# Ten of 64 context projections of a cross-attention moved into an expert layer's scatter and gather, and kept in HBM

## The chip, the cores and the metric

The kernel runs on one core of a Trainium2 chip, in one launch. The metric is the device time of the core in microseconds. The engines are TensorE (PE, with its weight loads listed as PEld), VectorE (DVE), ScalarE (ACT), GpSimd (POOL) and SyncE (SP), which only issues DMAs here.

## The reference

Two transformer layers run on 8 sequences of 100 tokens with 512 features (800 tokens), with a context of 8 x 722 rows. Everything is float32.

```
x = x + xattn0(layernorm(x), ctx)      # 16 heads of 32; causal: only the first 100 context rows count
x = x + experts0(layernorm(x))         # 8 experts of 2048, the best 2 per token, GELU
x = x + xattn1(layernorm(x), ctx)      # 16 heads of 64, below
x = x + experts1(layernorm(x))         # 8 experts of 1024, the best 2 per token, SiLU gate

xattn1:  q = xn @ Wq;  k, v = xn @ Wkv
         mem = ctx @ Wm                # 512 -> 1024; serves as keys and as values
         attn = softmax(q . [k, mem] / 8);  out = (attn . [v, mem]) @ Wo + bo
```

The part that matters is `mem = ctx @ Wm`. It depends on the context and on a weight alone, not on anything that earlier stages compute.

## The kernel before, in words

The kernel is written with a tile framework that places the semaphores and orders the instructions of each engine; the order in which they run is not always that of the source. Tiles come from pools. Tiles of one tag share `bufs` places, and a new tile waits until the old one in its place has been read for the last time. Memory of a closed pool is given to the next pool in the same way.

The stages run one after the other:

1. First attention (L407 to L513). `cT` (the context), `kT` and `v` are its large tiles in the pool `ap`. The last part of the stage (L535 to L550) is the output projection, the layer norm and the router's logits for each of seven tiles of tokens.
2. Routing (L552 to L573). `places` ranks the tokens of each expert. `owners` reads the order of the experts into SP's registers, since the weights' addresses depend on it. `weights.load` then fetches the first two weight tiles, and `send` scatters the rows to HBM with 14 indirect DMAs on POOL.
3. First expert layer (L576 to L623). `work_off` goes through eight jobs, one per expert. `arrive` loads the rows (`xg`) and turns them, `hidden` and `product` are the two matmul stages, and `send_back` (the function `returned`) stores the answers. `weights.get` keeps loads seven tiles ahead on SP. Behind the jobs stands `rest` (L378), a branch that every engine passes and that is taken only when an expert overflows. Then 28 indirect gathers (`fetch`, L317) add the answers to `x` (L621).
4. Second attention (L626 to L778). After a layer norm (L634 to L638) come the queries `qT` (L645), and then 64 units, 8 batches times 8 blocks `ic` of two heads each. Batch 0 and batch 4 begin with the keys `kT` for four batches, and each batch with its `v` (L750) and with the load of its context `cb` (L739).
5. Second expert layer (L781 to L869), built as the first.

In a unit of the second attention, `keys` (L649) projects 128 columns of `mem` for all 722 context rows: 2 halves of 4 accumulating matmuls (L655), each evicted by ScalarE (L661). The result `mT` has features on partitions. `values` (L664) turns it with six PE transposes (L671) and three VectorE copies into `mv`, with rows on partitions. `weighed` (L679) makes scores (L689), the maximum (L693) and the exponentials (L695). `turned` transposes the probabilities (L710 to L716) and `attended` multiplies them with `mv` (L725 to L734). The loop is staggered by one unit:

```
mT = keys(cb, ic)
if before is not None:
    turn = turned(*before[4])
mv = values(mT)
here = b, ic, v, mv, weighed(b, ic, kT, mT)
if before is not None:
    attended(*before[:4], *turn)
```

Of the kernel before, what the change touches and what calls it, by code (L numbers as in the profile page):

```python
# [8 lines left out]
F32 = mybir.dt.float32  # L9
# [4 lines left out]
P = 128  # L14
D = 512
DC = D // P
B, T, S = 8, 100, 722
NT = B * T
HALF = NT // 2
NTILE = -(-NT // P)  # L20
# [4 lines left out]
IC = INNER // P  # L25
# [3 lines left out]
NKH = NK // 2  # L29
EPS = 1e-5  # L30


# [30 lines left out]
def two_layers(ctx: ExitStack, tc: tile.TileContext, a: dict, out: bass.AP):  # L63
# [151 lines left out]
    sent = dram.tile([ROWS, D], F32, name="sent")  # L215
    answers = dram.tile([ROWS, D], F32, name="answers")

    def places(at1, at2, pool, psum, tag, name):
# [145 lines left out]

    def work_off(jobs, arrive, hidden, product, send_back, first=None):


        (x, raw), done = arrive(*jobs[0][:3]), None
        if first is not None:
            weights.load(first + 8, raw)  # L370
        for k, (e, r0, n, w1, w2) in enumerate(jobs):
            h = hidden(e, n, x, w1, lambda: done and send_back(*done))
            if k + 1 < len(jobs):
                x, _ = arrive(*jobs[k + 1][:3])
            done = e, r0, n, product(e, n, h, w2)
        send_back(*done)
# [16 lines left out]
    def columns_part(dst, xT, w, h, c, psum, evict):  # L393
# [8 lines left out]
        evict(dst[:, c, cols], ps[:, :HALF])  # L402


    f0 = ctx.enter_context(ExitStack())
    fp = f0.enter_context(tc.tile_pool(name="f0", bufs=1))
    with tc.tile_pool(name="a0", bufs=1) as ap, tc.tile_pool(name="a0w", bufs=3) as aw, tc.tile_pool(  # L407
        name="a0s", bufs=1, space=bass.MemoryType.PSUM
    ) as ps_s, tc.tile_pool(name="a0p", bufs=2, space=bass.MemoryType.PSUM) as ps:
        w_q = weights.get(0, 0)  # L410
        cT = ap.tile([P, DC, B, T], F32, name="cT")
        for dc, queue in enumerate((nc.gpsimd, nc.gpsimd, nc.sync, nc.sync)):
# [7 lines left out]
        make_causal_mask(nc, mask, -1e30)  # L420
        nil = ap.tile([P, 1024], F32, name="nil")
        nc.gpsimd.memset(nil, 0.0)
# [15 lines left out]
        qT = ap.tile([P, DC, NT], F32, name="qT0")  # L438
        kT = ap.tile([P, DC, NT], F32, name="kT0")
        v = ap.tile([T, B, D], F32, name="v0")  # L440

# [84 lines left out]
        nc.vector.tensor_tensor(wg0, wg0, gamma0.unsqueeze(2).to_broadcast([P, DC, NE]), ALU.mult)  # L526
        xl = fp.tile([P, NTILE, D], F32, name="xl0")
        xT = ap.tile([P, DC, NT], F32, tag="xT", name="xTf0")
# [31 lines left out]
        weights.load(W_L0F + 2)  # L560
        send(xl, where, "f0")
        b1s = by_order(hot, b1.rearrange("p e f -> p f e"), F0 // P, fp, "b1")
        b2s = by_order(hot, b2T, DC, fp, "b2")
# [12 lines left out]
    with f0, tc.tile_pool(name="f0w", bufs=2) as fw, tc.tile_pool(  # L576
        name="f0p", bufs=2, space=bass.MemoryType.PSUM
    ) as ps:
        NF = F0 // P

        def hidden0(e, n, xg, w1, between):
            h = fw.tile([P, NF, CAP], F32, tag="h", name="h0")
            for g in range(NF // 4):
# [13 lines left out]

        def work0(jobs, first=None):
            work_off(
                jobs, lambda e, r0, n: arrived(e, r0, n, fw, ps, gamma0, beta0), hidden0,  # L600
                lambda e, n, h, w2: products(n, h, [w2(g) for g in range(NF // 4)], NF, fw, ps, b2s[:, e, :]),
                lambda e, r0, n, yT: returned(e, r0, n, yT, fw, ps), first,
            )
# [6 lines left out]
            for e in range(NE)  # L610
        ], W_L0F)
        rest(
            more, work0, lambda piece, e, g: piece(of(0, "W1", e, g)), lambda piece, e, g: piece(of(0, "W2", e, g)), 4
        )

        for i in range(NTILE):
            w = rows[i]
# [8 lines left out]
    with tc.tile_pool(name="a1", bufs=1) as ap, ExitStack() as later, tc.tile_pool(  # L626
# [21 lines left out]

        def keys(cb, ic):  # L649

            mT = aw.tile([P, S], F32, tag="mT", name="mT")
            for h in range(2):
                pm = ps.tile([P, 512], F32, tag="tp", name="ps_m")
                for dc in range(DC):
                    nc.tensor.matmul(  # L655
                        pm[:, : S // 2],
                        w_m[ic // 4][:, dc, (ic % 4) * P : (ic % 4 + 1) * P],
                        cb[:, dc, h * (S // 2) : (h + 1) * (S // 2)],
                        start=dc == 0, stop=dc == DC - 1,
                    )  # L660
                nc.scalar.copy(mT[:, h * (S // 2) : (h + 1) * (S // 2)], pm[:, : S // 2])  # L661
            return mT

        def values(mT):  # L664

            mv = aw.tile([P, NSC, P], F32, tag="mv", name="mv1")
            for c0, c1 in ((0, 4), (4, NSC)):
                pt = ps.tile([P, 4, P], F32, tag="tp", name="ps_mv")
                for c in range(c0, c1):
                    w = min(P, S - c * P)  # L670
                    nc.tensor.transpose(pt[:w, c - c0, :], mT[:, c * P : c * P + w], ident)  # L671
                if c1 < NSC:
                    nc.vector.tensor_copy(mv[:, c0:c1, :], pt)
                else:
                    nc.vector.tensor_copy(mv[:, c0 : c1 - 1, :], pt[:, : c1 - 1 - c0, :])
                    nc.vector.tensor_copy(mv[:SLAST, c1 - 1, :], pt[:SLAST, c1 - 1 - c0, :])
            return mv
# [79 lines left out]
        for n in range(B * IC):  # L757
            b, ic = divmod(n, IC)
            if ic == 0:
                cb, kT, v = batch(b, kT)  # L760
            mT = keys(cb, ic)
            if before is not None:
                turn = turned(*before[4])
            mv = values(mT)
            here = b, ic, v, mv, weighed(b, ic, kT, mT)
# [174 lines left out]
```

## Time and profile before

| what | value |
|---|---|
| median of three runs | 1920.64 us (1918.02 to 1923.47) |
| the profiled execution | 1925.57 us, its span 1923.5 us |
| instructions | 26011 |
| mean granted TensorE clock | 0.944 of full |
| PE busy | 1731.2 us (90% of the span) |
| VectorE, ScalarE, POOL busy | 583.6, 459.8, 153.8 us |
| DMA | 203.19 MB, mean 106 GB/s |

The page of a profile gives busy time per engine, then the span in 40 slices of some 48 us with the busy share of each engine in tenths, the granted TensorE clock, and the DMA share. Groups of instructions are named by line, engine and operation, with the tiles that they write and read. A view of windows gives the busy time of each engine in chosen stretches. A timeline lists instructions in order of time; in brackets stands the idle time before one and what ended it. The stages lie about here: first attention to 210 us, routing and scatter to 247, expert jobs to 635, gather and layer norm to 682, second attention to about 1510, second expert layer to the end.

### The profile page before, as it was taken

How to read it: one execution, taken by the hardware profiler on the slowest of the kernel's cores; microseconds unless marked ns; L12 is line 12 of the kernel's file. 1: busy time of each engine (PE TensorE's matmuls, PEld its weight loads, DVE VectorE, ACT ScalarE, POOL GpSimd, SP SyncE). 2: the span in 40 equal slices, each digit the busy share in tenths (PEclk: the TensorE clock that was granted, in tenths of full speed). 3: DMA queues.
4: the chain of work that ended last, by engine and by line, in shares of the span. 5: the costliest groups of instructions: out<-in, count | busy, mean ns of one | idle time of the engine just before them, and what ended most of it. 6: DMA issues, size and time to landing. Idle time of an engine off the chain costs nothing. (4 is left out here: it accounts for less than half of the span.)

```text
span 1923.5 us, 26011 instructions
## 1 busy us (share of the span) xinstructions
PE 1731.2 (90%) x10442; PEld 1312.4 (68%) x10442; DVE 583.6 (30%) x1409; ACT 459.8 (24%) x1359; POOL 153.8 (8%) x262
## 2 busy tenths in 40 slices
PE   4999389999999289999999999999999939999990
PEld 2455179999999255666666656666666428999990
DVE  2465410011110411444444424444434221111115
ACT  2364111111111022333333323333333010010110
POOL 2000210000000310000000000000000040000003
PEclk9997689999999689999999999999999959999995
DMA  9800274545554520000000000000000046455623
GB/s 334 334 2 1 106 265 167 188 177 193 210 200 190 170 84 22 1 32 1 32 6 27 32 1 1 32 7 26 1 1 1 11 166 249 166 189 200 209 80 111
DMA packets 44202, 203.19 MB, mean 106 GB/s; under 512 B 8490, under 2 KB 8618, under 8 KB 27938
## 3 DMA queue, kind: packets, MB, share of 16 engines
q1 hardware_dynamic: 27904, 158.54, 22.5%
q0 software_dynamic: 8992, 27.93, 4.2%
q10 hardware_dynamic: 7170, 14.91, 2.3%
q8 instruction: 86, 1.41, 0.3%
q14 instruction: 50, 0.41, 0.1%
HBM read 162.21 MB, written 39.13 MB: 105 GB/s over the span
## 5 line engine op out<-in xcount | busy, mean ns | idle before, releaser
L655 PE MATMUL ps_m<-cb,w 128*128 128x361 f32 x1024 | 327.0, 471 | 0.0
L341 PE MATMUL ps_y<-h,w 128*128 128x256 f32 (+7 forms) x1536 | 280.5, 344 | 0.0
L341 PEld LDWEIGHTS ps_y<-h,w 128*128 128x128 f32 x1536 | 268.6, 190 | 7.9
L655 PEld LDWEIGHTS ps_m<-cb,w 128*128 128x128 f32 x1024 | 188.9, 189 | 114.1 <-issue 4.6
L589 PE MATMUL ps_h<-xgT,w 128*128 128x256 f32 (+7 forms) x1024 | 188.8, 345 | 0.0
L589 PEld LDWEIGHTS ps_h<-xgT,w 128*128 128x128 f32 x1024 | 180.2, 191 | 5.7 <-ACT h L593 0.2
L695 ACT ACTIVATE pr<-ps_sc,m 100x822 f32<-100x822 f32 x128 | 120.0, 943 | 194.8 <-DVE m L693 194.8
L711 DVE COPY prT<-ps_ptA 128x500 f32<-128x500 f32 x128 | 82.0, 679 | 232.2 <-PE ps_ptA L710 232.1
L693 DVE TENSOR_REDUCE m<-ps_sc 100x1 f32<-100x822 f32 x128 | 123.8, 1009 | 45.8 <-PE ps_sc L689 45.8
L593 ACT ACTIVATE h<-ps_h,s_b 128x256 f32<-128x256 f32 (+7 forms) x128 | 56.1, 439 | 303.6 <-PE ps_h L589 303.6
L661 ACT COPY mT<-ps_m 128x361 f32<-128x361 f32 x128 | 59.2, 462 | 246.4 <-PE ps_m L655 246.4
L398 PE MATMUL ps_col<-xT,w 128*128 128x400 f32 x320 | 116.0, 521 | 0.0
L819 PE MATMUL ps_g<-xgT,w 128*128 128x256 f32 (+7 forms) x512 | 104.3, 347 | 0.0
L819 PE MATMUL ps_u<-xgT,w 128*128 128x256 f32 (+7 forms) x512 | 102.8, 344 | 0.0
L398 PEld LDWEIGHTS ps_col<-xT,w 128*128 128x128 f32 x320 | 62.3, 198 | 46.5 <-issue 5.1
L819 PEld LDWEIGHTS ps_g<-xgT,w 128*128 128x128 f32 x512 | 91.3, 192 | 3.0
L819 PEld LDWEIGHTS ps_u<-xgT,w 128*128 128x128 f32 x512 | 90.7, 190 | 2.7
L689 PE MATMUL ps_sc<-mT,qT 64*100 64x311 f32 (+1 forms) x512 | 89.2, 466 | 0.0
L719 POOL COPY wide<-sums 100x128 f32<-100x128 f32 x64 | 19.0, 296 | 779.9 <-DVE sums L700 779.9
L731 PE MATMUL ps_av<-prT,mv 128*64 128x100 f32 (+1 forms) x1536 | 80.6, 253 | 0.0
L825 DVE TENSOR_TENSOR h<-ps_u,sg 128x256 f32<-128x256 f32 (+7 forms) x64 | 24.3, 380 | 183.8 <-PE ps_u L819 183.8
L824 ACT ACTIVATE sg<-ps_g 128x256 f32<-128x256 f32 (+7 forms) x64 | 22.3, 349 | 238.8 <-PE ps_g L819 238.8
(219 smaller groups left out, 1853.1 us busy)
## 6 DMA issues: line engine op xcount, KB each, us to landing
w<-in_W SPq DMA_DIRECT2D x64, 1024.0 KB, 6.6
w<-in_w_gate SPq DMA_DIRECT2D x16, 1024.0 KB, 4.8
w<-in_w_up SPq DMA_DIRECT2D x16, 1024.0 KB, 7.3
w<-in_w_down SPq DMA_DIRECT2D x16, 1024.0 KB, 6.7
sent<-nil SPq DMA_DIRECT2D x25, 512.0 KB, 10.1
cb<-in_ctxT ACTq DMA_DIRECT2D x8, 1444.0 KB, 6.2
answers<-nil SPq DMA_DIRECT2D x19, 512.0 KB, 9.9
xg<-sent POOLq DMA_DIRECT2D x18, 256.0 KB, 4.8
```

The costliest lines, as they stand in the source:

```text
L341: nc.tensor.matmul(py[:, k, :n], ws[f // 4][:, f % 4, dc * P : (dc + 1) * P], h[:, f, :n], start=f == 0, stop=f == nf - 1,)
L398: nc.tensor.matmul(ps[:, :HALF], w[c // 4][:, dc, (c % 4) * P : (c % 4 + 1) * P], xT[:, dc, cols], start=dc == 0, stop=dc == DC - 1,)
L589: nc.tensor.matmul(ph[:, :n], w[:, dc, j * P : (j + 1) * P], xg[:, dc, :n], start=dc == 0, stop=dc == DC - 1,)
L593: nc.scalar.activation(h[:, f, :n], ph[:, :n], AF.Gelu, bias=b1s[:, e, f : f + 1])
L655: nc.tensor.matmul(pm[:, : S // 2], w_m[ic // 4][:, dc, (ic % 4) * P : (ic % 4 + 1) * P], cb[:, dc, h * (S // 2) : (h + 1) * (S // 2)], st ...
L661: nc.scalar.copy(mT[:, h * (S // 2) : (h + 1) * (S // 2)], pm[:, : S // 2])
L689: nc.tensor.matmul(sc[:, bank, c0:c1], qT[r, ic, q0 : q0 + T], keys_, start=True, stop=True)
L693: nc.vector.tensor_reduce(m, sc[:, :, :NKH], AX.XY, ALU.max, negate=True)
L695: nc.scalar.activation(pr.rearrange("p (a n) -> p a n", a=2), sc[:, :, :NKH], AF.Exp, bias=m, accum_out=sums[:, j : j + 1],)
L711: nc.vector.tensor_copy(prT[:, : NSC - 1, :], pt)
L731: nc.tensor.matmul(po[r, 0, :], vj, prT[j][:w, c, :], start=c == 0, stop=c == NSC)
L819: nc.tensor.matmul(p_[:, :n], w_[:, dc, j * P : (j + 1) * P], xg[:, dc, :n], start=dc == 0, stop=dc == DC - 1,)
```

## The change

For batches 0 and 1, the blocks `ic` = 0, 1, 3, 5 and 7 are done early, ten units in all. Their `mT` and `mv` go to two tensors in HBM, `kept_keys` and `kept_values`, by ScalarE's DMA queue. In the second attention these units load both back on SP in place of projecting and turning; `mv` needs two loads, since the last of its six row blocks has 82 rows.

Batch 0's five projections stand in the source after `send`. Their weights and context are loaded on SP into the places of `cT`, `kT` and `v`. Batch 1's five stand after `rest`, ahead of the gathers. Their weights and context are loaded by POOL from inside job 4 of the expert layer, behind one-element copies that wait for a row tile. For the memory, the expert layer's `h` has one buffer in place of two. In the second attention, where a kept unit is followed by one that is not kept, half of the next unit's projection is placed in the kept unit.

```diff
+EARLY = ((0, 1, 3, 5, 7), (0, 1, 3, 5, 7))
+KEPT = {(b, ic): (b * len(EARLY[0]) + k) for b in range(len(EARLY)) for k, ic in enumerate(EARLY[b])}
...
+    def moved(dma, mv, kept, store):
+        for part in ((slice(0, P), slice(0, NSC - 1)), (slice(0, SLAST), slice(NSC - 1, NSC))):
+            here, there = mv[part[0], part[1], :], kept[part[0], part[1], :]
+            dma(out=there if store else here, in_=here if store else there)
+
+    def project_early(b, cb, w_m, tiles, psum, tags):
+        for ic in EARLY[b]:
+            mT, mv = tiles()
+            context_columns(mT, ic, cb, w_m, psum, tags[0])
+            nc.scalar.dma_start(out=kept_keys[KEPT[b, ic]], in_=mT)
+            context_rows(mv, mT, psum, tags[1], nc.scalar.copy)
+            moved(nc.scalar.dma_start, mv, kept_values[KEPT[b, ic]], True)
...
         owners(0, experts)
         weights.load(W_L0F + 2)
         send(xl, where, "f0")
+        w_m = []
+        for g, tag in enumerate(("cT", "kT")):
+            w_m.append(ap.tile([P, 4, 512], F32, tag=tag, name=f"wm0{g}"))
+            nc.sync.dma_start(out=w_m[g], in_=a["Wm"][g])
+        cb = ap.tile([P, DC, S], F32, tag="v", name="cb0")
+        nc.sync.dma_start(out=cb, in_=a["ctxT"][:, 0, :].rearrange("(c p) s -> p c s", p=P))
+        project_early(
+            0, cb, w_m, lambda: (
+                ap.tile([P, S], F32, tag="nil", name="mT0", bufs=2), aw.tile([P, NSC, P], F32, tag="xn", name="mv0")
+            ), ps, ("tp", "av"),
+        )
...
+        def fetch_context(behind):
+
+            for t, src in (
+                (w_m[0], a["Wm"][0]), (w_m[1], a["Wm"][1]),
+                (cb, a["ctxT"][:, 1, :].rearrange("(c p) s -> p c s", p=P)),
+            ):
+                nc.gpsimd.tensor_copy(t[:1, 0, :1], behind[:1, 0, :1])
+                nc.gpsimd.dma_start(out=t, in_=src)
...
-            h = fw.tile([P, NF, CAP], F32, tag="h", name="h0")
+            h = fw.tile([P, NF, CAP], F32, tag="h", name="h0", bufs=1)
...
+        project_early(
+            1, cb, w_m, lambda: (
+                fw.tile([P, S], F32, tag="xgT", name="mT1"), fw.tile([P, NSC, P], F32, tag="xg", name="mv1")
+            ), ps, ("m", "tp"),
+        )
         for i in range(NTILE):
             w = rows[i]
...
+            if (b, ic) in KEPT:
+                nc.sync.dma_start(out=mT, in_=kept_keys[KEPT[b, ic]])
+            else:
+                context_columns(mT, ic, cb, w_m, ps, "tp", (0, 1) if first and whole else (0,) if first else (1,))
             return mT
...
+            if (b, ic) in KEPT:
+                moved(nc.sync.dma_start, mv, kept_values[KEPT[b, ic]], False)
+            else:
+                context_rows(mv, mT, ps, "tp", nc.vector.tensor_copy)
             return mv
...
-            mT = keys(cb, ic)
+            mT = keys(b, ic, cb)
+            if (b, ic) in KEPT and ic + 1 < IC and (b, ic + 1) not in KEPT:
+                keys(b, ic + 1, cb, whole=False)
             if before is not None:
                 turn = turned(*before[4])
-            mv = values(mT)
+            mv = values(b, ic, mT)
```

`context_columns` and `context_rows` are the former bodies of `keys` and `values`, with the halves and the engine of the copies as arguments.

## The prediction

> **What bounds the kernel now.** I read the page first, for which engine is busy in which slice, then windows cut at the stage borders, then TensorE's timeline inside one unit of the second attention.
>
> ```profile
> PE 1731.2 (90%) x10442; PEld 1312.4 (68%) x10442; DVE 583.6 (30%) x1409; ACT 459.8 (24%) x1359; POOL 153.8 (8%) x262
> PE   4999389999999289999999999999999939999990
> PEclk9997689999999689999999999999999959999995
> ```
>
> PE is busy 90% of the span, and full in every slice but a few. Its holes are the strips where tokens are routed, scattered or gathered; the clock row dips in the same places. The change moves PE work out of a full stretch into two of the holes, so the windows (columns: window, length, then busy us of PE, PEld, DVE, ACT, POOL, clock, DMA share, GB/s) have to show how much hole there is:
>
> ```profile
> 175.00:208.00 33.00, 29.82 (x126) 16.94 (x124) 15.13 (x56) 11.07 (x24) 0.00 (x0) 1.00 0.00 0
> 208.00:217.00 9.00, 1.94 (x17) 1.72 (x17) 5.72 (x38) 2.53 (x5) 0.00 (x0) 0.55 0.00 0
> 217.00:225.00 8.00, 0.57 (x3) 0.38 (x2) 7.17 (x26) 0.00 (x0) 0.53 (x1) 0.50 0.00 0
> 225.00:244.00 19.00, 0.00 (x0) 0.00 (x0) 0.00 (x0) 0.00 (x0) 13.02 (x14) 0.50 0.77 284
> 640.00:669.00 29.00, 0.49 (x3) 0.52 (x4) 15.51 (x32) 0.98 (x4) 15.18 (x14) 0.50 0.56 168
> 750.00:1500.00 750.00, 749.19 (x5157) 488.93 (x5156) 311.43 (x602) 249.19 (x716) 18.96 (x64) 1.00 0.04 13
> ```
>
> From 750 to 1500, the second attention, PE is idle for 0.8 us in 750 and the clock is 1.00: a matmul taken out there comes off the time. In the routing and scatter strip (208 to 244) and the gather strip (640 to 669) PE stands still at clock 0.50. The DMA engines are empty until 225, then 77% busy.
>
> TensorE inside the second attention (start, busy, engine, line, tile):
>
> ```profile
> 998.31 0.87 PE L671 MATMUL ps_mv<-ident,mT 128*128 128x128 f32 x6
> 999.12 0.42 PE L689 MATMUL ps_sc<-kT,qT 64*100 64x100 f32 x4
> ...
> 1000.68 0.31 PE L725 MATMUL ps_av<-ident,wide 100*128 100x100 f32 x1
> ...
> 1002.28 5.12 PE L655 MATMUL ps_m<-cb,w 128*128 128x361 f32 x16
> 1007.24 0.59 PE L710 MATMUL ps_ptA<-ident,pr 100*128 100x100 f32 x5
> ...
> 1011.30 0.30 PE L725 MATMUL ps_av<-ident,wide 100*128 100x100 f32 x1
> ```
>
> A unit takes 1011.30 - 1000.68 = 10.62 us. The projection (L655) holds PE from 1002.28 to 1007.24, 4.96 us by start to start; its turning (L671) from 998.31 to 999.12, 0.81 us. Together 5.77 us.
>
> **Part 1, what is removed.** Ten units lose both: 10 x 5.77 = 57.7 us. The work also covered a wait. The scores of a unit end as 1000.68 begins, and its softmax rows come from these two:
>
> ```profile
> 1001.89 0.95 ACT L695 ACTIVATE pr<-ps_sc,m 100x822 f32<-100x822 f32 x1 [3.03 <-DVE m L693]
> 1002.83 0.94 ACT L695 ACTIVATE pr<-ps_sc,m 100x822 f32<-100x822 f32 x1
> ```
>
> They are there at 1002.84 and 1003.77. PE has `attended` of the unit before (1000.68 to 1002.28), then the projection, then `turned`, which needs them. Without a projection PE would wait to 1002.84, turn the first (0.6), and wait 0.3 again: 0.9 us. At ic = 1, 3 and 5 the change puts half of the next projection (2.5 us) there, and at ic = 0 the batch's values (L750, 6.9 us from 748.69 to 755.55) stand there; only ic = 7 is bare: 2 x 0.9 = 1.8 us. Net **-55.9 us**. VectorE loses three copies in each of these units and ScalarE two, but both have slack (311 and 249 busy us of 750), so I cost that at nothing.
>
> **Part 2, the loads back.** Each of the ten units puts three loads on SP, 370, 328 and 42 KB, 30 in all. SP does nothing between the second `Wo` load (issued at about 727.7) and the end of this stage. The first is needed when scores start, about 755. Later ones may start when the tile two units back is freed and are needed about 14 us on (a step of some 8 us and most of one of 7). Nearest rows: a 1024 KB weight lands in 6.6 us, a 1444 KB `cb` in 6.2. A load that waits on SP holds up only later loads of this kind. Taken: 0. Bounds: no gain is possible; the cover ends at a landing of 14 us, and each us beyond costs up to 10.
>
> **Part 3, five projections in the scatter strip.** PE needs 5 x 5.77 = 28.9 us at full clock. What decides is when they may start. `wm` and `cb` lie in the places of `cT`, `kT` and `v`, free after the last `attended0` (about 170); DMA is idle there, so 3.5 MB land by about 177. But in the code their SP loads stand after `owners` and two weights, which issue at 225.43. Does the order on an engine follow the code? No:
>
> ```profile
> 163.18 0.41 PE L480 MATMUL ps_pt<-ident,pr 100*100 100x100 f32 x1
> 163.38 1.96 PE L541 MATMUL ps_o<-w,qT 128*128 128x512 f32 x2
> 165.13 0.37 PE L480 MATMUL ps_pt<-ident,pr 100*100 100x100 f32 x1
> ```
>
> Output projections (L541) run between transposes of attention units that the code puts before them, and the `cb` load of L739 is issued at 689.78 among the evictions of L647. Instructions are ordered by when their inputs are ready, so I take the loads and matmuls to move ahead. Then the cover is PE's idle time from 177 to the first `xg` transposes at 247.43: about 3 + 7.1 + 7.4 + 22.4 = 40 us, against 28.9 us. Slots of 0.3 us may push routing matmuls back: +1 (0 to 5). The stores, 5 x 0.74 MB on ScalarE's queue, fall partly into 225 to 244: some 2.2 MB at the 378 GB/s this trace reaches are 5.9 us, where 23% of 19 = 4.4 us are free: +1. ScalarE has 5 x (2 x 0.46 + 1.1) us of copies and 15 issues of some 0.4, all below PE's 28.9. Taken: **+2 us**; bounds -3 (experts starting on a warm clock) and +8.
>
> **Part 4, fetching for batch 1.** Three copies and three DMA issues on POOL inside the expert layer. POOL idles 15 to 30 us between its issues there, and one copy with one issue is about 1 us. Behind them on POOL stand the `answers` stores and `xg` loads, issued 17 to 30 us apart. The 3.5 MB run beside weights at some 190 GB/s; with 150 left they need 24 us, and weights are loaded seven ahead. `h` with one buffer: PE has finished `product` before the next `hidden` writes it. Taken: 0; bounds 0 and +3.
>
> **Part 5, five projections in the gather strip.** The last matmul before the strip ends at 634.84, the next is at 668.51. PE passes a branch first. ScalarE's row shows what a branch costs and what a cold clock costs:
>
> ```profile
> 614.54 0.41 ACT L593 ACTIVATE h<-ps_h,s_b 128x176 f32<-128x176 f32 x1 [0.78 <-PE ps_h L589]
> 620.37 1.28 ACT L133 ACT_TABLE_LOAD   x1 [5.42 <-ACTq L381]
> ...
> 687.09 0.50 ACT L647 ACTIVATE qT<-ps_col 128x400 f32<-128x400 f32 x1 [4.28 <-PE ps_col L398]
> 689.78 0.50 ACT L647 ACTIVATE qT<-ps_col 128x400 f32<-128x400 f32 x1 [2.18 <-PE ps_col L398]
> ```
>
> 5.42 us at the branch puts PE's start at 640.3. By then the clock is at 0.5: the first `qT` group took 681.5 to 687.0, 5.4 us, the next 2.69, so a cold start costs 2.7 us. The Trainium skill (TensorE: Matmul & The Clock Gate, Part 1: The HAM clock gate) speaks against work put into such a strip: after an idle window of about 3.4 us PE runs at half rate, and needs about 3.4 us of sustained work to recover, a loss of 1.7 us. I take the row, 2.7, as it is this place; with the rule the total would be 1.0 less. Were the clock never to recover, each group would cost 57.7 us. End on PE: 640.3 + 28.9 + 2.7 = 671.9.
>
> ScalarE's copies wait on PE there, and behind them stand the square roots of the next layer norm (first at 653.03), for which VectorE waits; they cost nothing as long as the strip ends on PE anyway. Then the next stage must get its memory: `xn` at 667.87 and the `bo` load at 667.96 both came just after the last reader of the old buffers (667.73). Now the last store must land too: copies and issue, 1.5 us, then the landing. By the skill (DMA: Bandwidth & Descriptors, Anatomy of one DMA) about 2.0 us plus bytes over 436 GB/s, 2.9 us for 370 KB, an estimate; the trace's nearest row, `answers<-y` into HBM, 256 KB, has 6.6, on a busier queue. They give 676.3 and 680.0, that is +8.6 or +12.3 against 667.73, or only +3.4 if the memory does not overlap. Taken: **+8 us**, near the rule, because DMA is emptier at the end of the strip; the row would make the total 4 more. Bounds -3 (`qT` on a warm clock) and +14.
>
> **Sum.** -55.9 + 2 + 8 = -45.9. The profiled execution took 1925.57 us (span 1923.5, 2.1 around it): 1879.7. The median of the runs is 1920.64, 4.9 lower: **1875**.
>
> **The rivals.** (a) Half saved: kept units wait on softmax or loads, some 2 us each, 20 in all: 1895. For it: VectorE and ScalarE need 3.1 us between scores and probabilities. Against it: 4 us of cover in eight of ten units. (b) In series: the loads keep their place behind `owners`. Weights 2.1, scatters 3.3 and context 3.5 MB at some 365 GB/s from 225.4 end at about 250; 28.9 + 2.7 + 3 us on PE and to store put the first `xg` transposes at 284.6, 37 us late in place of 2: 1910. For it: the code's order. Against it: the rows above. (c) Slower: as (b), and the clock stays at 0.50 as in those windows, since PE waits on copies between matmuls. Then 57.7 us from 250 and 3 to store end at 311, 64 late: 1937. It decides once the first experts start more than 48 us late, after 295. Against it: the clock was back at 1.00 by 256 when L589 began. (d) Nothing changes: if gaps gave back all 56 us by chance, about 1921.
>
> **How the numbers follow.** Main case 0.66 (own range 1860 to 1888), (a) 0.13, (b) 0.10, (c) and mishaps of its size 0.08, (d) 0.03. The range 1859 to 1908 takes in the low bounds, (a) and half of (b); outside stay (c), (d), half of (b) and a little below. About 0.3% (6 us) is what a measurement can tell from no change. Faster is main, (a) and (b), 0.89; same 0.03; slower 0.08.
>
> **What would show it.** Right: projection matmuls starting near 177 to 210 and ended before 245; first `xg` transposes by 252; clock 1.00 from 210 to 238; ten units of about 5 us (or pairs of half) less; the first `qT` matmul at about 690. Wrong: `wm` and `cb` loads after 225; PE waiting on DMA `mT` or `mv` in the kept units; transposes of `xn` after 690; probabilities as releaser of `turned` in more than the two bare units.

## The result, and the profile after

The changed kernel takes 1889.26 us (median of four runs, 1887.25 to 1891.05), the kernel before 1921.31 us in the same comparison. The ratio is 0.9834, with a 95% interval from 0.9817 to 0.9852: 32 us are gone. The forecast was 1875 us, in a range from 1859 to 1908. Its direction and range held; the gain is 14 us smaller than its point.

First the page of the changed kernel, the same three rows as were shown of before.

```profile
PE 1738.8 (92%) x10442; PEld 1315.2 (70%) x10442; DVE 572.9 (30%) x1379; ACT 468.5 (25%) x1389; POOL 154.6 (8%) x268
PE   4999969999999979999999999999999939999990
PEclk9997889999999979999999999999999959999995
```

PE's instruction count is unchanged, 10442: nothing was saved, work was moved. The two dips are the holes. In the fifth and sixth slice, the scatter strip, the PE row has 9 and 6, where it had 3 and 8; in the 14th and 15th, the gather strip, it has 9 and 7, where it had 2 and 8. The windows at the same borders as before (window, length, then busy us of PE, PEld, DVE, ACT, POOL, clock, DMA share, GB/s), with two added behind the borders, since both strips end later now:

```profile
208.00:217.00 9.00, 9.00 (x24) 4.97 (x24) 4.71 (x32) 2.26 (x5) 0.00 (x0) 0.51 0.00 0
217.00:225.00 8.00, 8.00 (x35) 5.23 (x34) 3.57 (x16) 2.40 (x6) 0.00 (x0) 1.00 0.21 81
225.00:244.00 19.00, 16.51 (x68) 10.36 (x66) 3.63 (x11) 6.42 (x18) 11.79 (x12) 1.00 0.86 319
244.00:256.00 12.00, 0.58 (x3) 0.61 (x4) 0.00 (x0) 1.28 (x1) 4.71 (x12) 0.50 0.71 254
640.00:669.00 29.00, 22.25 (x81) 14.35 (x80) 7.88 (x15) 6.07 (x15) 11.32 (x12) 0.88 0.78 264
669.00:686.00 17.00, 11.60 (x48) 7.26 (x46) 8.87 (x19) 4.78 (x14) 3.99 (x4) 0.95 0.61 218
```

PE fills the holes. Three things are new beside that. From 208 to 217 PE is busy all the time and the clock is still 0.51, so nearly all of these 24 matmuls run at half speed. The DMA engines are busy for 86% of 225 to 244. And a second hole has opened at its end: from 244 to 256 PE does 0.58 us of work.

Cut at marks that both kernels have, the spans differ like this. R is the first `ps_b2T` transpose, where the routing begins.

| stretch | before | after | difference |
|---|---|---|---|
| start to R | 169.68 | 167.87 | -1.8 (varies from profile to profile) |
| scatter strip: R to the first `xg` transposes | 77.75 | 87.55 | +9.8 |
| expert jobs, to the last `ps_yt` transposes | 386.00 | 385.82 | -0.2 |
| gather strip: to the first `xn` transposes | 35.08 | 44.83 | +9.75 |
| layer norm, to the first `qT` matmul | 13.01 | 13.25 | +0.2 |
| second attention, to the first full `ps_o` group | 802.54 | 750.80 | -51.7 |
| the rest | 439.44 | 439.18 | -0.3 |

The sum is -34.2 us, the difference of the spans (1923.5 and 1889.3). So 51.7 us came out of the attention and 19.6 us were paid back in the two strips, where 10 had been expected. Both columns are one profiled execution each.

**Scatter strip.** SyncE's own queue shows that the loads did move ahead of `owners`, whose weights are the third row:

```profile
138.15 22.91 SPq L609 DMA_DIRECT2D wm<-in_Wm  x2
168.00 0.39 SPq L611 DMA_DIRECT2D cb<-in_ctxT  x1
230.09 0.92 SPq L57 DMA_DIRECT2D w<-in_W  x2
```

TensorE's timeline then shows what the early projections (L416) met. The logits (L171) and the ranks (L236) are routing work, for which the scatter waits:

```profile
207.70 2.77 PE L416 MATMUL ps_m<-cb,wm 128*128 128x361 f32 x4
210.40 0.60 PE L171 MATMUL ps_lg<-p_Wg,xTf 128*32 128x8 f32 x8
210.93 0.27 PE L175 MATMUL ps_lg<-p_bg,ones 1*32 1x8 f32 x2
211.13 9.74 PE L416 MATMUL ps_m<-cb,wm 128*128 128x361 f32 x22
220.70 0.33 PE L236 MATMUL ps_rank_f<-before_f,every 128*128 128x64 f32 x2
```

Twenty-two projection matmuls stand in PE's queue between the last logits and the ranks. They take 9.57 us by start to start, where 22 x 0.31 = 6.8 us is the price at full clock. In the kernel before, PE was idle at this place and waited for VectorE:

```profile
216.46 0.69 PE L231 MATMUL ps_rank_f<-before_f,every 128*128 128x64 f32 x2 [5.53 <-DVE before_f L229]
```

Measured from R, the ranks come at 52.83 us in place of 46.78, 6 us late. Much of this is the clock: the 26 projection matmuls from 207.70 on lost 4.2 us to it (the working stands in the last section). An estimate from this: at full clock the ranks would have been some 2 us late. Then GpSimd's timeline has the end of the strip, in which `xg` is the load that the first expert waits for; the first row is the kernel before, the other two are the changed kernel:

```profile
244.08 2.26 POOL L329 DMA_DIRECT2D xg<-sent  x4 [2.09 <-issue]
245.43 0.86 POOL L313 DMA_INDIRECT sent<-xl,whole_f  x1 [0.31 <-issue]
252.19 2.27 POOL L334 DMA_DIRECT2D xg<-sent  x4 [5.90 <-DMA kept_values<-mv]
```

Before, POOL was idle for 2.09 us ahead of this load. Now it is idle for 5.90, and a store of `kept_values` ends that. `xg` is the first tile of a new pool, in the memory of the closed one, so it can wait until the last store out of that memory has landed; that this is the reason is inferred here, and the run with own buffers below supports it. The first scatter starts 5.5 us later after R than before, the 14 scatters take 0.6 us longer, and the wait is 3.8 us longer: these make the 9.8.

**Gather strip.** ScalarE's timeline, and then PE's:

```profile
655.80 1.28 ACT L136 ACT_TABLE_LOAD   x1
662.61 0.29 ACT L136 ACTIVATE rb<-mv_a,eps 128x1 f32<-128x1 f32 x1 [5.53 <-DVE mv_a L128]
662.81 0.44 ACT L420 COPY mT<-ps_m 128x361 f32<-128x361 f32 x1
```

```profile
650.34 0.69 PE L428 MATMUL ps_mv<-ident,mT 128*128 128x128 f32 x2 [3.20 <-ACT mT L420]
663.30 0.66 PE L428 MATMUL ps_mv<-ident,mT 128*128 128x128 f32 x4 [3.55 <-ACT mT L420]
```

PE waits twice for a copy of `mT` by ScalarE. The first time the branch is in the way (ScalarE passes it only at 649.83). The second time a square root of the next layer norm stands on ScalarE ahead of the copy and itself waits 5.53 us for VectorE, which waits for gathers. VectorE's row shows what ended the strip; the first row is the kernel before, where the same work came right behind the last update of `x`:

```profile
667.87 1.00 DVE L142 TENSOR_SCALAR xn<-x,rb,tb 128x512 f32<-128x512 f32 x2
685.47 1.00 DVE L145 TENSOR_SCALAR xn<-x,rb,tb 128x512 f32<-128x512 f32 x2 [4.38 <-DMA kept_values<-mv]
```

Again the landing of the last store. But the gathers are late too: measured from the last `ps_yt` transposes, the last update of `x` comes at 38.29 us, before at 33.58. The view of the tile `back` gives the time from the issue of a gather to its landing, first before, then after, for the 14 gathers of this strip (28 is the number for both expert layers):

```profile
DMA to landing us min/median/max: 2.6/3.6/3.9
DMA to landing us min/median/max: 3.5/5.2/6.4
```

From the first gather's issue to the last update of `x` pass 26.4 us in place of 21.2.

### The profile page after: what moved, and what is told of

The parts are those of the page before. It is cut to its first block, busy times and chain, and to the rows that moved or that the text cites. A ratio compares the mean times of both kernels' runs of the same rounds, so it can differ in the third digit from the quotient of the medians.

```text
span 1889.3 us, 26129 instructions
## 1 busy us (share of the span) xinstructions
PE 1738.8 (92%) x10442; PEld 1315.2 (70%) x10442; DVE 572.9 (30%) x1379; ACT 468.5 (25%) x1389; POOL 154.6 (8%) x268
## 5 line engine op out<-in xcount | busy, mean ns | idle before, releaser
L416 PE MATMUL ps_m<-cb,w 128*128 128x361 f32 x864 | 277.6, 472 | 0.0
L416 PEld LDWEIGHTS ps_m<-cb,w 128*128 128x128 f32 x864 | 158.9, 189 | 95.5 <-issue 3.6
L773 PEld LDWEIGHTS ps_ptA<-ident,pr 100*128 100x128 f32 x640 | 65.0, 140 | 21.6 <-issue 10.4
```

Source lines behind the costliest of these rows:

```text
L416: nc.tensor.matmul(pm[:, : S // 2], w_m[ic // 4][:, dc, (ic % 4) * P : (ic % 4 + 1) * P], cb[:, dc, h * (S // 2) : (h + 1) * (S // 2)], st ...
L773: nc.tensor.transpose(pt[:, c, :], pr[:, T + c * P : T + (c + 1) * P], ident[:T, :T])
```

## The experiments

The kernel before took 1920.5 to 1921.1 us beside these runs. Since the start to R alone was 162.6 to 169.7 us from profile to profile with the same code, and five runs of one kernel spread over 5 to 9 us, differences of 3 us between two variants are read from the strips of their profiles, not from the times. Each strip is read from one profile of its kernel. Four kernels with the same code in the scatter strip lie within 0.7 us there (+9.8 to +10.5), but three with the same code in the gather strip lie 5 us apart (+6.2, +9.75, +11.5), so smaller differences in the gather column show a direction at best. The differences to the kernel before, in us:

| kernel | time | scatter strip | gather strip | layer norm | attention |
|---|---|---|---|---|---|
| the full change | 1889.26 | +9.8 | +9.75 | +0.2 | -51.7 |
| batch 0 alone | 1904.70 | +10.0 | 0.0 | -0.2 | -26.3 |
| batch 1 alone | 1903.66 | -0.1 | +6.2 | 0.0 | -26.0 |
| batch 0, own buffers | 1904.83 | +11.1 | +0.4 | -0.3 | -26.5 |
| projections behind the ranks | 1892.73 | +10.3 | +11.5 | +0.1 | -51.9 |
| square roots last | 1885.77 | +10.5 | +7.4 | -0.5 | -51.3 |
| eight units | 1892.12 | +7.6 | +7.3 | -0.2 | -44.4 |
| values of `ic` = 7 not kept | 1891.45 | +9.1 | +8.2 | -0.5 | -51.3 |
| eight units, square roots last | 1894.12 | +7.8 | +4.8 | -0.3 | -43.3 |
| first unit's stores alone | 1880.90 | +5.5 | +7.3 | -0.5 | -52.0 |
| the same, square roots last by ScalarE | 1880.72 | +3.9 | +4.5 | +2.0 | -52.3 |
| no values of 7, square roots last by ScalarE | 1888.13 | +9.7 | +4.8 | +2.2 | -52.1 |
| square roots last by ScalarE | 1890.19 | +10.1 | +6.8 | +2.2 | -51.6 |

**One strip at a time.** Batch 0's units alone, and batch 1's alone; the other batch's loads, projections and stores are not there.

```diff
-EARLY = ((0, 1, 3, 5, 7), (0, 1, 3, 5, 7))
+EARLY = ((0, 1, 3, 5, 7), ())   # or ((), (0, 1, 3, 5, 7))
```

> Only batch 0's five units are kept; batch 1 is as before. Theory S (the cost sits in each strip by itself: queue order on PE, ScalarE and the release of the old pool): the second attention gives 25.9 us, the scatter strip takes 9.8 back, so about 16 us less than before, 1905; the first xg transposes at about 255 as with the full change. Rival R (the strips disturb each other through DMA: kept stores, context loads inside the expert layer and weights share bandwidth): without batch 1's loads and stores the scatter strip or the expert jobs get shorter by several us, below 1902.

> Only batch 1's five units are kept; batch 0 is as before. Theory S: 25.9 us gained in the second attention, 10.0 lost in the gather strip, about 1905, the first xg transposes back at 247 and those of xn about 10 us later than before (678). Rival R: the loss in the gather strip shrinks or grows by more than 3 us without batch 0's part.

Measured were 1904.70 us, ratio 0.9923 (0.9903 to 0.9944), and 1903.66 us, 0.9918 (0.9901 to 0.9935). Each half brings half of the gain, and each strip pays in its own kernel alone: a strip without early work is the strip of before within 0.2 us. The scatter strip costs the same alone as in the full change (10.0 and 9.8), as theory S had it. The gather strip costs 6.2 us alone and 9.75 in the full change. That is 3.5 us less, more than the 3 us that were named as the sign of rival R. It could be the variation of that strip, or something of batch 0's part that reaches it; which of the two was not tried.

**Own buffers for batch 0.** In the kernel with batch 0 alone, `mT` and `mv` get places in a pool that stays open until the experts end, one buffer each.

```diff
-ap.tile([P, S], F32, tag="nil", name="mT0", bufs=2), aw.tile([P, NSC, P], F32, tag="xn", name="mv0")
+fp.tile([P, S], F32, tag="mTe", name="mT0"), fp.tile([P, NSC, P], F32, tag="mve", name="mv0")
```

> As the run with batch 0 alone, but the early mT and mv lie in the pool f0, which stays open through the expert layer, one buffer each. Theory S (the first xg load waits until every store of the closed pool has landed): the load is issued when the scatters have landed, about 248 in place of 252, or when PE ends, if one buffer makes PE wait for stores; 1 to 4 us better than batch 0 alone. Rival R (bandwidth delays the xg load): no change, or worse by PE's waits for the single buffers.

Measured: 1904.83 us, ratio 0.9934 (0.9909 to 0.9959), and a strip of +11.1. With one buffer each, ScalarE waits 1.9 to 6.7 us for the store of the unit before at every unit but the first, and PE ends 84.1 us after R in place of 74.2. So the edit brought a new wait in the place of the one that it was to remove. GpSimd's timeline of this kernel still tells something:

```profile
246.01 2.27 POOL L334 DMA_DIRECT2D xg<-sent  x4 [4.80 <-ACT mT L420]
251.61 0.77 POOL L56 COPY w<-xg 1x1 f32<-1x1 f32 x6 [3.33 <-DMA xg<-sent]
```

The `xg` load no longer waits for a store, and it is issued 1.6 us sooner after R than with batch 0 alone, as theory S had it. But then GpSimd waits 3.33 us for it to land, where it waits 0.81 with batch 0 alone, so the stores that are still under way may hold it up in another way, as rival R had it.

**The projections behind the ranks.** Two one-row writes into `cb` that need the order of the experts hold the projections of batch 0 back until the ranks are computed.

```diff
 nc.sync.dma_start(out=cb, in_=a["ctxT"][:, 0, :].rearrange("(c p) s -> p c s", p=P))
+nc.vector.scalar_tensor_tensor(cb[:1, :, :1], hot[:1, 0, :DC].unsqueeze(2), 0.0, cb[:1, :, :1], ALU.mult, ALU.add)
+nc.vector.scalar_tensor_tensor(cb[:1, :, S // 2 : S // 2 + 1], hot[:1, 0, :DC].unsqueeze(2), 0.0, ...)
```

> The full change, but batch 0's context tile gets one VectorE touch that reads the routing result, so no early projection can stand ahead of the ranking matmul. Theory S (6 us of the loss are projections queued ahead of the ranking on PE at half clock): the first scatter is issued 6 us earlier, about 222; but PE then starts its 29 us at about 217 on a cold clock and ends at 250, the stores land at 258, and the first xg transposes move to about 261: 4 to 8 us slower than the full change, 1893 to 1897. Rival C (PE order is free, only the 29 us of PE work count): the first scatter stays at 228.

Measured: 1892.73 us, ratio 0.9859 (0.9840 to 0.9878). The ranks are on time again (46.78 us after R, as before), the scatter starts 53.29 after R, 7 us sooner than in the full change, and nothing is won. GpSimd's timeline of this kernel, the last scatter and the `xg` load:

```profile
234.69 0.86 POOL L313 DMA_INDIRECT sent<-xl,whole_f  x1 [0.31 <-issue]
249.42 2.27 POOL L334 DMA_DIRECT2D xg<-sent  x4 [13.87 <-DMA kept_values<-mv]
```

The 7 us are given back in the wait for the stores, 13.87 us long. The edit moves the projections too: PE ends 81.7 us after R in place of 74.3, so the stores come later as well. The strip is 0.5 us longer than in the full change, where theory S had it 4 to 8 us longer; rival C is refuted by the scatter's start. The stores and the routing are two paths to the same point, and this edit shortens one by lengthening the other.

**The stores left out.** Of a batch's five units only the first is stored, and its data are loaded in the place of the other four; the projections, turnings and loads all stay. The cut shows the stores; the loads are changed in the same way.

```diff
-            nc.scalar.dma_start(out=kept_keys[KEPT[b, ic]], in_=mT)
+            if ic == 0:
+                nc.scalar.dma_start(out=kept_keys[KEPT[b, 0]], in_=mT)
...
-            moved(nc.scalar.dma_start, mv, kept_values[KEPT[b, ic]], True)
+            if ic == 0:
+                moved(nc.scalar.dma_start, mv, kept_values[KEPT[b, 0]], True)
```

> Left out: of the five units of a batch only the first is stored; the other four are projected and turned as before and never stored, and in the attention stage all five kept units of a batch load the first one's keys and values (the same loads, other data). So 3.0 of 3.7 MB of stores are gone from each strip, and nothing else. Theory T (the stores' traffic and their landing carry part of both strips): in the scatter strip the wait of the xg load for the stores goes and the late routing matmuls stay, +6 in place of +9.8; in the gather strip the last update of x comes 34 to 35 us after ps_yt as in the kernel before, not 38.3, and then TensorE's end (39.7 after ps_yt) decides: +5.5 in place of +9.8. In all 8 us sooner: 1880 to 1883. Rival P (TensorE's work and its late start set both ends, the stores merely land meanwhile): within 2 us of the full change, 1887 to 1890.

Measured: 1880.90 us, ratio 0.9792 (0.9779 to 0.9805), where the full change has 0.9834 (0.9817 to 0.9852): the stores cost some 8 us of device time, of which the two strips of the profiles show 6.7 (4.3 and 2.4). Theory T had put it at 1880 to 1883. GpSimd's timeline of this kernel:

```profile
245.41 0.86 POOL L313 DMA_INDIRECT sent<-xl,whole_f  x1 [0.30 <-issue]
248.35 2.27 POOL L334 DMA_DIRECT2D xg<-sent  x4 [2.08 <-issue]
```

The wait is 2.08 us, that of the kernel before. The strip still costs 5.5 us, since the ranks are as late as in the full change (52.95 after R). That settles the scatter strip: the stores are worth 4.3 us of it, and what is left is the late routing (the first scatter starts 5.6 us later than before). In the gather strip VectorE's row shows the other end:

```profile
679.95 1.01 DVE L145 TENSOR_SCALAR xn<-x,rb,tb 128x512 f32<-128x512 f32 x2 [4.67 <-ACT mv L433]
```

No store ends the wait now. It is ScalarE's last copy behind PE, which ended 40.93 us after `ps_yt`. Theory T had PE's end at 39.7; it came 1.2 us later, so the strip kept 7.3 us, not 5.5. The last update of `x` came at 36.41, not at 34 to 35 as expected, but it does not set the end here.

**The square roots behind the last `mT`.** The next layer norm's square roots read a bias that is written once the last `mT` of the gather strip (`last` in the cut) is there, so none can stand ahead of an `mT` copy. VectorE writes it in one version and ScalarE in another.

```diff
+        nc.vector.scalar_tensor_tensor(eps3, last[:, S - 1 :], 0.0, eps2, ALU.mult, ALU.add)
...
-scaled(xn, x[:, i, :], *factors(moments(x[:, i, :], "a1"), "b", twice=True))
+scaled(xn, x[:, i, :], *factors(moments(x[:, i, :], "a1"), "b", twice=True, bias=eps3))
```

> All ten units kept; the square roots of the next layer norm read a bias that is written only after the last mT of the gather strip, so that none stands on ScalarE ahead of an mT copy. In the changed kernel one such square root waited 5.53 us for VectorE and TensorE then waited 3.55 us for its copy (at 663.30). Theory Q (ScalarE's queue sets when TensorE ends, and that sets the end of the strip): that wait is gone, TensorE ends about 3.5 us sooner, the first xn transposes come 3 to 4 us sooner, 1885 to 1886. Rival L (the landing of the last stores behind the gathers sets the end): 1889, the strip still 44 to 45 us. Rival D (the square roots and the scaling behind them, now all after the last mT, become the end): 1890 to 1893.

> All ten units kept whole; the square roots of the next layer norm read a bias that ScalarE writes after the last mT, where the earlier version had VectorE write it, which did so only at 680.46, behind the last update of x. Theory G (the gathers, slowed by the stores, set the end once TensorE is out of the way): the square roots come at about 675, the first xn at once after the last update of x, about 1 us sooner than in the earlier version: 1884 to 1886. Rival S (it was ScalarE and VectorE around the square roots that held xn up): 3 us sooner or more, 1881 to 1883.

Measured with VectorE: 1885.77 us, ratio 0.9802 (0.9784 to 0.9821). PE ends 34.71 us after `ps_yt` in place of 39.69: the wait on ScalarE's queue was real, and worth 5 us of PE. The strip becomes only 2.4 us shorter. VectorE's timeline of this version says why:

```profile
679.79 0.74 DVE L696 SCALAR_TENSOR_TENSOR x<-back,m_f,x 32x512 f32<-32x512 f32 x1 [0.97 <-DMA back<-answers,whole_f]
680.46 0.14 DVE L690 SCALAR_TENSOR_TENSOR eps<-mT,eps 128x1 f32<-128x1 f32 x1
680.96 0.16 DVE L140 RECIPROCAL rb<-rb 128x1 f32<-128x1 f32 x1 [0.36 <-ACT rb L137]
681.67 0.55 DVE L146 TENSOR_SCALAR xn<-x,rb,tb 128x512 f32<-128x512 f32 x1 [0.27 <-DVE rb L140]
```

The last update of `x` waits for a gather (`back`) until 679.79, which is 39.95 us after `ps_yt`, and all else follows within 2 us. The gathers have become the end. Neither theory had this: theory Q had the strip 3 to 4 us shorter, and rival L named the landing of the stores, with a strip as long as in the full change. With ScalarE writing the bias the measurement is 1890.19 us, ratio 0.9831 (0.9813 to 0.9849), no better than the full change. By the marks the first `xn` transposes come 0.6 us sooner than with VectorE, but the layer norm behind them takes 15.2 us in place of 12.6. Its last square root, at 695.77, now stands behind the `xT` evictions on ScalarE, and VectorE waits 2.99 us for it. Theory G's place for the end is right, its 1 us was lost again two steps on, and rival S is refuted.

**Both together.** The stores of four units left out as above, and the square roots bound by ScalarE's bias.

> The same part left out (four of five units of a batch are not stored, the first one's data are loaded in their place), and the next layer norm's square roots bound behind the last mT by a bias that ScalarE itself writes. Theory T and Q together: nothing of the stores is left in the gather strip and TensorE ends about 35 us after ps_yt, as early as the gathers: that strip costs 1 to 2 us over the kernel before, the scatter strip 6: 1876 to 1879. If TensorE's work costs time in a strip even when it ends in time and nothing is stored (by the clock, the branch or ScalarE's queue): 1881 to 1884. It bounds what this change could give with its transfers free.

Measured: 1880.72 us, ratio 0.9792 (0.9776 to 0.9809), the same as without the bound square roots. The gather strip falls to +4.5, and the layer norm takes 2 us more. Expected were +1 to +2; that is refuted. PE ended at 36.49 and the last update of `x` came at 36.8. But the edit had put a table load and square roots ahead of ScalarE's last copies of `mv`, so memory came free only at 672.27, 38.5 us after `ps_yt`. So with nearly all stores gone the strip still costs 4.5 us, a part of which this edit brought; how large a part was not tried.

**Fewer units, and a smaller last store.** Four units a batch without `ic` = 7; then all ten, but of `ic` = 7 only the keys; then each with the bound square roots.

```diff
+EARLY = ((0, 2, 4, 6), (0, 2, 4, 6))
```

```diff
     nc.scalar.dma_start(out=kept_keys[KEPT[b, ic]], in_=mT)
+    if ic == IC - 1:
+        continue
     context_rows(mv, mT, psum, tags[1], nc.scalar.copy)
```

> Eight units in place of ten: ic = 0, 2, 4, 6 in both batches, so that ic = 7 keeps its projection in the attention stage and no kept unit is bare. Theory P (a kept unit is worth 5.65 us, the two bare ones lost 1.8 us each and the two first of the batch 1 us; a strip costs by its work: TensorE's end, half clock and backlog of stores): attention saves about 8 x 5.65 = 45.2 less 1 to 2, the scatter strip costs 6 to 8 and the gather strip 4 to 7 in place of 10 and 10: 1885 to 1889, no worse than ten units. Rival F (the strips' costs are fixed, paid for starting at all): 20 us of strips stay, saving 8/10 of 52 to 45: 1896 to 1899.

> All ten keys kept, but of ic = 7 the values are neither turned nor stored early; they are turned from the kept mT in the attention stage. Theory B (the bare unit of ic = 7 loses because TensorE waits for its probabilities, and the last value stores are what the end of both strips waits for): the turning of 0.81 us comes back in two units but falls into the wait of 0.6 us, so attention loses 0.4 to 1 us in all at most; both strips lose one turning and end on the smaller and earlier store, 2 to 4 us sooner each: 1883 to 1887. Rival L (the stores' backlog as a whole or the gathers set the end): 1889 to 1891.

> Eight units (ic = 0, 2, 4, 6 of both batches) and the square roots bound to the last mT of the gather strip. If theories P and Q both hold, the gains add as far as the gather strip still ends on TensorE: 1882 to 1886. If with four units a strip no longer ends on TensorE, the square roots cost nothing or cost their own length after it: the same as eight units alone, or up to 3 us more.

> All ten keys kept, values of ic = 7 turned in the attention stage, and the square roots bound behind the last mT by a bias that ScalarE writes. By the profiles of the two parts: scatter strip 0.7 us, gather strip 2.4 + 1 us, and the next layer norm 0.7 us sooner than in the full change, attention 0.4 us longer: 1884 to 1886. If the stores' traffic sets the end of the gather strip more than their number and the last one's size, no better than the full change with the square roots bound alone: 1885 to 1887.

Eight units: 1892.12 us, ratio 0.9845 (0.9827 to 0.9862). Attention saves 44.4 us, 5.55 a unit, 7.3 us less than with ten. Leaving two units out gave back 2.2 and 2.45 us in the strips. So a fifth less work made the strips 22% and 25% cheaper: rival F, with fixed costs, is refuted, and the strips behave about as theory P had it (6 to 8 us and 4 to 7 us were expected, +7.6 and +7.3 came). Its total of 1885 to 1889 was missed all the same: the two units left out saved 7.3 us and gave back 4.65 in the strips. Keys alone for `ic` = 7: 1891.45 us, 0.9841 (0.9824 to 0.9858); by the strips 0.7 and 1.5 us better, by the times not to be told from the full change, and above the 1883 to 1887 that theory B gave. Eight units with bound square roots: 1894.12 us, 0.9861 (0.9841 to 0.9881), the second of its two expectations (up to 3 us above eight units alone). By the profiles, against the full change attention loses 8.4 us, and the two strips and the layer norm win 7.5. Ten with keys alone and bound square roots: 1888.13 us, 0.9834 (0.9821 to 0.9848), above both of its expectations and the same as the full change, since the layer norm pays 2.2 us as in the other kernels with ScalarE's bias. The lowest median of a kernel that does all the work is 1885.77, with the square roots bound by VectorE; its interval overlaps that of the full change, so that it is faster is not shown.

## Why the prediction was right, and where its steps were off

- **What bounds the kernel: right.** In the second attention a matmul taken out comes off the time. That part gave 51.7 of the 55.9 us.
- **Part 1, -55.9, measured -51.7.** The mechanism was right, and terms were mis-sized. Compared from unit to unit in the two profiles, six kept units with cover save 5.66 us each, nearly the 5.77. But the two bare units save 3.98 us each, where 5.77 - 0.9 = 4.87 was reckoned, and the first two units of batch 0 together 10.46 us, 1.1 less than 2 x 5.77, though a cover stands there. These are 3.5 of the 4.2 us. (In both kernels the end of a batch has one unit that is 0.4 us longer; this is set aside.) TensorE's timeline of the changed kernel, first a kept unit with cover and then a bare one (a unit ends with the start of an L788 row):

```profile
793.47 0.59 PE L773 MATMUL ps_ptA<-ident,pr 100*128 100x100 f32 x5
795.02 1.39 PE L752 MATMUL ps_sc<-mT,qT 64*100 64x311 f32 x8
796.34 0.30 PE L788 MATMUL ps_av<-ident,wide 100*128 100x100 f32 x1
...
819.31 0.30 PE L788 MATMUL ps_av<-ident,wide 100*128 100x100 f32 x1
820.63 0.34 PE L794 MATMUL ps_av<-prT,v 100*64 100x100 f32 x4
821.61 0.65 PE L773 MATMUL ps_ptA<-ident,pr 100*128 100x100 f32 x5 [0.64 <-ACT pr L758]
822.61 0.69 PE L752 MATMUL ps_sc<-mT,qT 64*100 64x311 f32 x2
823.23 0.65 PE L773 MATMUL ps_ptA<-ident,pr 100*128 100x100 f32 x5
824.23 1.38 PE L752 MATMUL ps_sc<-mT,qT 64*100 64x311 f32 x5
825.54 0.31 PE L788 MATMUL ps_av<-ident,wide 100*128 100x100 f32 x1
```

  The wait on the probabilities (0.64) is there as foreseen. What was left out is that the transposes and scores behind it are slower as well: 3.93 us from 821.61 to the end of the unit, where the unit with cover takes 2.87 from 793.47. In the bare unit the scores run in parts, with the transposes between them, and in the first pair of batch 0 they do too (3.89 us). Why they take longer so was not tried.
- **Part 2, the loads back, 0: right.** No `mT` or `mv` load ends a wait of PE in that stage. Rival (a) is refuted: kept units with cover save nearly all of their 5.77 us, and among the kept units probabilities hold up `turned` only in the two bare ones, by 0.64 us each.
- **Part 3, +2 (-3 to +8), measured +9.8: the step that failed.** Its first half, that the loads and matmuls move ahead, was right, and rivals (b) and (c) with their loads behind `owners` are refuted by the SP queue. But the same freedom let projections into PE's queue ahead of the routing matmuls, and "slots of 0.3 us" were 22 matmuls in a row: the ranks came 6 us late, where 1 was reckoned. The half clock, at which the first of them ran, stood nowhere in this part's sum (the prediction had the clock at 1.00 from 210 on); it lost 4.2 us. And the cover was reckoned as PE's idle time. What ended the strip was the stores in a full DMA system: 1 us reckoned, 3.8 measured as the longer wait and 4.3 by leaving the stores out.
- **Part 4, 0: right.** The expert jobs take 385.8 us in place of 386.0, with one `h` and with the fetch in them.
- **Part 5, +8, measured +9.75: near in size, and partly by another way.** PE was to end 38.5 us behind `ps_yt` and ended at 39.69; from there to the release 4.4 us were given, and 4.5 measured. But the first unit's matmuls ran ahead of the branch, at full clock. Then PE waited 3.20 us for ScalarE at the branch and 3.55 us for a square root in ScalarE's queue. The prediction had named those square roots and costed them at nothing; it looked at who waits for them, not at who stands behind them. So it is in part luck that PE's end came out so near: PE started 6.4 us sooner than reckoned, and 6.75 us of waits were not reckoned. For the landing the Trainium skill (DMA: Bandwidth & Descriptors, Anatomy of one DMA) gave an estimate of 2.9 us for 370 KB and the trace's row 6.6; taken was near the rule. The page states its fit for DMAs that GpSimd issues, while these stores go by ScalarE's queue, so it is no more than a neighbour. The last store, a piece of 41 KB, was issued at 681.9 at the latest and released `xn` at 685.47: 3.6 us.
- **The sum.** Against the profiled execution, 11.4 us are missing (1891.05 and 1879.7): 4.2 of Part 1, 7.8 of Part 3 and 1.75 of Part 5 make 13.8, less 2.1 in the other stretches, above all the shorter start; 0.3 stay over. The other 3 us are in the medians: that of before lay 4.9 us below its profiled execution, that of after only 1.8.
- **The signs named.** The projections ran from 207.7 to 242.2, as named. The first `xn` transposes came by 690, but the first `xg` transposes came at 255.4 in place of 252, the clock was not at 1.00 from 210 to 217, and the first `qT` matmul came at 699 in place of 690.

## What to carry to other kernels

To move work into an engine's hole, ask of every queue in the hole what will stand behind the work, not only whether the engine is idle: here part of the cost came from routing matmuls behind projections on PE, and from `mT` copies behind square roots on ScalarE. A hole in one engine can be the busy time of another resource. The DMA engines were already 77% busy in the scatter strip, and what the moved work had to write came on top.

When a strip ends on three paths within some us of each other, to shorten one wins less than it takes away: 7 us from the scatter's start, bought with later stores, won nothing, and 5 us from PE's end in the gather strip won 2.4 in the one profile of it. Measure what is left by taking the largest suspect out whole, as the stores here.

## What the runs showed of the hardware

- The clock stayed at half for about 9 us under unbroken work. In the full change PE is busy for all of 208 to 217 us, with matmuls of 128 x 361 but for 0.7 us of logits, and the clock is 0.51; it is 1.00 only behind that. The prediction weighed 2.7 us of loss against an estimate of 1.7 by the Trainium skill (TensorE: Matmul & The Clock Gate, Part 1: The HAM clock gate), which has about 3.4 us of sustained work until the clock is back. Here 26 matmuls from 207.70 lost 2.70 - 4 x 0.31 = 1.5 and 9.57 - 22 x 0.31 = 2.75 us, 4.2 in all. With the projections behind the ranks, a start after 2.81 us of idle time took 7.45 us for 16 matmuls in place of 4.96, a loss of 2.5. Why these differ is open.
- Stores took longer to land where the DMA engines were busier. With these busy for 95 to 100% from 230 to 250 us, the last stores of the scatter strip landed some 7.5 us after their issue; in the gather strip, with the engines busy for under 50% from 680 us on, the last landed after 3.6 us.
- Gathers took longer to land beside the stores: a median of 3.6 us in the kernel before, 5.2 in the full change, and 3.8 in the kernel without four of five stores, with all else in it. From the first gather to the last update of `x` passed 21.2, 26.4 and 22.9 us.
- The gather strip with the same code in it cost 6.2 us in one kernel, 9.75 and 11.5 in others, along with the last update of `x` (34.9, 38.3 and 39.5 us behind `ps_yt`). What sets this difference was not tried.
